# A four-layer graph network on one core: layer 2's clamps on POOL, its squares between two exponentials, and the rows' tangent from an exponential

## The chip, the core and the metric

The kernel runs on one core of one Trainium2 chip. The metric is the device time of one execution in microseconds (us). Engines are named as in the profile: PE is TensorE's matmul, PEld its weight load, DVE is VectorE, ACT is ScalarE, POOL is GpSimd, SP is SyncE.

## What is computed

A vector of 64 features for each of 4096 nodes passes four graph layers. Each layer normalizes the rows of x, clips them at zero, mixes them over a 4096x4096 adjacency matrix, and adds the result to x.

```python
h = jnp.maximum(_layernorm(x, axis=-1), 0.0)
x = x + _L2_gnn_ref(h, adj, L2_gnn_weight, L2_gnn_bias)
```

Layer 0 is a sum over neighbours with a linear map, layer 1 an attention with a sigmoid weight for each pair of nodes, and layer 3 a sum over each node's last 100 neighbours. The change is in layer 2, which takes a logarithmic map between each pair of nodes on the Poincare ball, sums it with the adjacency as weight, applies a linear map, and goes back with an exponential map:

```python
arg = jnp.clip(sqrt_c * sub_norm, 0.0, TANH_CLIP)
return 2.0 / (sqrt_c * lam_x) * jnp.arctanh(arg) * sub / sub_norm
...
agg = jnp.einsum('ij,ijc->ic', w, log_ij)
transformed = agg @ weight + bias
...
second = jnp.tanh(sqrt_c * lam_x * v_norm / 2.0) * v / (sqrt_c * v_norm)
```

Around the origin the last line is tanh(|v|) v / |v|, one tanh per row.

## The kernel before, in words

The nodes are cut into eight blocks of 512 (ib). A group is one block of 512 targets against 256 sources: a tile of 128 partitions x 2 chunks x 512, 1024 elements a partition, and 512 KB of the adjacency matrix. Layers 0, 1 and 3 have 128 groups each.

Layer 2 uses that the pair weight is symmetric but for the adjacency. Its list `work` (line 957) holds only the groups with source block J not below target block ib: 72 groups, 56 of them with J above ib ("two"), whose weights are also transposed on PE and weighed a second time for the other half. Eight groups ("cut") work on half a tile. A group goes through these steps:

- `l2_dists` (PE): float32 and bfloat16 matmuls into the PSUM tile mm give the distance expression;
- `l2_squares` (ACT): v is the square of mm; then `l2_signs` (PE) adds a term to mm;
- `l2_clamps` (line 1032, DVE): v is lowered by a constant and held above a small one, in place;
- `l2_roots` (line 1050, ACT): Ln of v in place, then t = exp(v/2), then v = exp(-v/2) in place;
- `l2_coshs` (DVE): t = max(mm, c) + t, after which mm is free; `l2_logs` (ACT): Ln of t;
- `l2_pairs` (DVE): t = min(t, top) * v; `l2_weights` (DVE): w = t * adj;
- `l2_turns` (PE) transposes t into PSUM; `l2_weights2` (DVE): two multiplies of 128x512 with the other half of the adjacency;
- `l2_sums` and `l2_sums2` (PE) add into the two accumulators; `l2_gathers` moves the turned half into the tile others.

When a target block has its last sum, `after2` (line 613) handles its rows: transposes, the linear map, the squared norm n, on POOL the powers n^0.5 and n^-0.5 by one `pow` of 128x8 (r_nn), on ACT the tanh of the norm, a reload of ACT's tables by `log_exp_tables` (line 297), and on DVE the product and the add to x. `before3` (line 532) follows with the next layernorm, whose inverse root is a POOL `pow` of 128x4 (ln_r), an add of a bias to x on POOL, and the bfloat16 splits for layer 3.

The order in which each engine gets its instructions is fixed when the kernel is built. `in_turn` (line 709) takes among generators the step that can start earliest by a model of times (`Pace`, line 59): 1.65 for a `pow` on POOL, 0.3 + n/600 for its other work, 2.6 for a reload of the tables. The steps of layer 2 that share an engine are bound together by `in_steps` (line 1212): in step s each generator does the group s minus its offset, in the order listed. ACT's list is logs (one behind), roots (level), squares (one ahead); DVE's is clamps, pairs (one behind), weights (one behind), coshs, second weights (one behind). Row work is put between these steps where the model finds it ready. The tiles v and t of the groups share six buffers. Every engine instruction of the kernel goes through one helper, so that all stand at line 129 in the profile, and groups are told apart by tile names.

Of the kernel before, what the change touches and what calls it, by code (L numbers as in the profile page):

```python
# [13 lines left out]
AF = mybir.ActivationFunctionType  # L14
# [10 lines left out]
CB = W // P  # L25
# [111 lines left out]
def kernel(ctx: ExitStack, tc: tile.TileContext, a: dict, out: bass.AP):  # L137
# [156 lines left out]
    def rt(name, shape, dtype=F32):  # L294
        return rows.tile(shape, dtype, tag=f"{name}_{slot['now']}", name=name, bufs=1)

    def log_exp_tables():

        tc.keep_in_program_order(nc.scalar.preload_act_table_set("natural_log_exp_and_others"))
        pace.free["ACT"] += 2.6  # L300
# [312 lines left out]
    def after2(ib, acc, others, st):  # L613

        e = rows.tile([P, W], F32, tag="e", name="e")[0 : D + 1, :]
        if others is None:
            ACT.copy(e, acc[0 : D + 1, :])
        else:
            DVE.tensor_add(e, acc[0 : D + 1, :], others)
        st["acc_free"][0] = pace.latest  # L620
        ps = yield from by_row(e, D + 1)

        t = rt("l2", [P, CB, D])
        z = rt("r_n", [P, CB, 1])
        DVE.tensor_copy(z, ps[:, :, D : D + 1])
        h = HA[:, cs(ib), 0:D]
        hz = rt("r_sq", [P, CB, D])
        DVE.tensor_mul(hz, h, ps[:, :, 0:D])  # L630
        DVE.tensor_mul(t, ps[:, :, 0:D], Qc[:, cs(ib), :].to_broadcast([P, CB, D]))
        yield ON_V
        y = rt("r_m", [P, CB, 1])
        DVE.tensor_reduce(y, hz, AX.X, ALU.add)
        DVE.tensor_mul(y, y, Mc[:, cs(ib), :])
        DVE.tensor_add(z, z, y)
        DVE.tensor_mul(z, z, Fc[:, cs(ib), :])
        yield ON_V
        DVE.tensor_mul(hz, h, z.to_broadcast([P, CB, D]))
        DVE.tensor_sub(t, t, hz)  # L640
        vT = columns[slot["now"]]
        yield from transposed(t, D, vT[0:D, :])
        ps = yield from times(vT, W2, D, ON_S)
        tr = rt("hb", [P, CB, D])
        ACT.copy(tr, ps)
        hz = rt("r_sq", [P, CB, D])
        ACT.activation(hz, tr, AF.Square)
        yield ON_V
        n = rt("r_nn", [P, 2 * CB, 1])
        DVE.tensor_reduce(n[:, 0:CB, :], hz, AX.X, ALU.add)  # L650
        DVE.tensor_scalar(n[:, 0:CB, :], n[:, 0:CB, :], MIN_NORM * MIN_NORM, None, ALU.max)
        DVE.tensor_copy(n[:, CB :, :], n[:, 0:CB, :])

        POOL.tensor_tensor(n, n, halves["both"], ALU.pow)
        yield ON_S
        th = rt("r_c", [P, CB, 1])
        ACT.activation(th, n[:, 0:CB, :], AF.Tanh)
        log_exp_tables()
        yield ON_V
        DVE.tensor_mul(th, th, n[:, CB :, :])  # L660
        DVE.tensor_mul(tr, tr, th.to_broadcast([P, CB, D]))
        DVE.tensor_add(x[:, cs(ib), :], x[:, cs(ib), :], tr)
        yield ON_V
# [307 lines left out]
    def targets(d):  # L971
        return slice(d["ib"] * W + (OWN if d["cut"] else 0), (d["ib"] + 1) * W)


    def ago(items, k, n, what):

        return items[k - n].get(what) if k >= n else 0.0
# [44 lines left out]
    def l2_squares():  # L1022
        for k, d in enumerate(work):
            yield "ACT", lambda: latest(
                d.get("dist"), l1[2 * k - SIG].get("summed") if 2 * k < SIG else 0.0,
                ago(work, k, SIG // 2, "paired"),
            )
            d["v"] = pair_buffer("v")
            ACT.activation(part(d, d["v"]), part(d, d["ps"]), AF.Square)
            d["square"] = pace.latest  # L1030

    def l2_clamps():
        for d in work:
            yield "DVE", lambda: d.get("square")
            v = part(d, d["v"])
            DVE.tensor_scalar(v, v, -half, V_MIN, ALU.add, ALU.max)
            d["clamped"] = pace.latest

    def l2_signs():
# [10 lines left out]
    def l2_roots():  # L1050
        for k, d in enumerate(work):
            yield "ACT", lambda: latest(
                d.get("clamped"), opened.get("tables"),
                l1[2 * k + 1 - SIG].get("summed") if 2 * k < SIG else 0.0,
                ago(work, k, SIG // 2, "weighed"), ago(work, k, SIG // 2, "turned"),
            )
            d["t"] = pair_buffer("t")
            v = part(d, d["v"])
            ACT.activation(v, v, AF.Ln)
            ACT.activation(part(d, d["t"]), v, AF.Exp, scale=0.5)  # L1060
            d["root"] = pace.latest
            ACT.activation(v, v, AF.Exp, scale=-0.5)
            d["inverse"] = pace.latest

# [7 lines left out]
    def l2_logs():  # L1072
        for d in work:
            yield "ACT", lambda: d.get("read")
            ACT.activation(part(d, d["t"]), part(d, d["t"]), AF.Ln, scale=2.0 / SC)
            d["log"] = pace.latest

    def l2_pairs():
        for d in work:
            yield "DVE", lambda: latest(d.get("log"), d.get("inverse"))  # L1080
            t = part(d, d["t"])
            DVE.scalar_tensor_tensor(t, t, top, part(d, d["v"]), ALU.min, ALU.mult)
            d["paired"] = pace.latest

    def l2_weights():
        for k, d in enumerate(work):
            yield "DVE", lambda: latest(
                opened.get("second"), d.get("paired"), arrival(d), ago(work, k, 2, "summed")
            )
            if not d["cut"]:  # L1090
                d["w"] = w2["pool"].tile([P, G, W], F32, tag="w", name="w")
            DVE.tensor_mul(part(d, d["w"]), part(d, d["t"]), part(d, d["adj"]))
            d["weighed"] = pace.latest
            used(d)
# [104 lines left out]
    def l2_gathers():  # L1199
        for d in twos:  # L1200
            if d["half"] == 0:
                continue
            yield "DVE" if d["ib"] else "ACT", lambda: d.get("summed2")
            o, acc = w2["others"][:, ws(d["J"])], accs["turned"][0 : D + 1, :]
            if d["ib"] == 0:
                ACT.copy(o, acc)
            else:
                DVE.tensor_add(o, acc, o)
            st["acc_free"][1] = pace.latest
            d["gathered"] = pace.latest  # L1210

    def in_steps(*stages):


        parts = [next(stage[0], None) for stage in stages]
        for step in range(-1, len(work) + 3):
            for n, (gen, behind, many) in enumerate(stages):
                k = step - behind
                for _ in range(many(work[k]) if 0 <= k < len(work) else 0):
                    yield parts[n]  # L1220
                    parts[n] = next(gen, None)
# [132 lines left out]
    def l3_pass():  # L1354

        for n, pair in enumerate(pairs3):
            while rank_need(pair) is None:
                yield "PE", lambda: first_of(rank_need(pair), sum_need() if sums3 else None)
                if rank_need(pair) is None:
                    l3_sum()  # L1360
            yield "PE", lambda: rank_need(pair)
            l3_rank(pair)
            for _ in range(1 + n % 2):
                if sums3 and sum_need() is not None:
                    yield "PE", sum_need
                    l3_sum()
        while sums3:
            yield "PE", sum_need
            l3_sum()

    def l3_weights():
        n = 0
        for d in l3:
            if d["late"]:
                place, reader = late_at[d["k"]]
                yield "ACT", lambda: latest(d.get("ranked"), reader.get("signed"))
                d["w"] = place
            else:
                yield "ACT", lambda: latest(
                    d.get("ranked"), opened.get("third"),  # L1380
                    ago([e for e in l3 if not e["late"]], n, WT, "summed"),
                )
                d["w"] = now["w3"].tile([P, G, W], BF16, tag="wt", name="wt")
                n += 1
            ACT.activation(d["w"].bitcast(U16), d["ps"], AF.Relu)
            d["read"] = pace.latest
# [8 lines left out]
    def l3_sum():  # L1395
# [22 lines left out]
        if d["last"]:  # L1418
# [8 lines left out]
            (l2_dists(), -1, once), (l2_signs(), 0, once), (l2_sums2(), 2, if_two(1)),  # L1427
            (l2_turns(), 1, lambda d: 2 if d["two"] else 1), (l2_sums(), 1, once),
        ),
        in_steps((l2_logs(), 1, once), (l2_roots(), 0, once), (l2_squares(), -1, once)),  # L1430
        in_steps(
            (l2_clamps(), 0, once), (l2_pairs(), 1, once), (l2_weights(), 1, once),
            (l2_coshs(), 0, once), (l2_weights2(), 1, lambda d: 2 if d["two"] else 1 if d["first"] else 0),
        ),
        l2_gathers(), l3_weights(), l3_pass(), l3_counts(), l3_masks(),
        degree_sums(0, l0), degree_sums(1, l1), constants(),
    ])

# [44 lines left out]
```

## Time and profile before

| what | value |
|---|---|
| median of the runs shown | 1198.92 us (1196.69 to 1200.99, 3 runs) |
| the profiled execution, its own time | 1196.08 us |
| its span, first to last instruction | 1194.4 us |
| busy in the span | PE 1077.9 (90%), DVE 950.6 (80%), ACT 800.7 (67%), POOL 118.2 (10%) |
| layer 2, by its first square and its last sums | about 482 to 960 us |
| clamp v<-v on DVE, 128x1024 | 64 times, mean 684 ns |
| ACT table loads | 19 times, 1283 ns |

A busy time is the sum of an engine's instructions, and engines work at the same time. A line of a timeline gives start, duration, engine, operation, out<-in with shapes, and in brackets the idle time before it and whom it waited for. A line of waits gives who waited for whom: total us, times, longest. An operation's displayed duration overlaps the next one's start by some 0.1 us on ACT and DVE, so that what it costs its queue is read from start to start.

### The profile page before, as it was taken

To read this page: it belongs to the slowest core of one execution; us is meant where nothing else is said; L and a number is where in the kernel's file an instruction comes from. 1 tells how busy PE (TensorE), PEld (TensorE's weight loads), DVE (VectorE), ACT (ScalarE), POOL (GpSimd) and SP (SyncE) were. 2 spreads that over 40 slices of the span, in tenths; PEclk is the share of its full clock that TensorE was granted. 3 is DMA by queue.
4 is the path that set the end of the run, shared out by engine and by line. 5 is a ranking of instruction groups with operands and counts; after the bars stand their busy time and mean duration, and the time that the engine had idled before them with its cause. 6 is when DMAs were issued, how large, how long until landed. Compare 5 with 4: busy or idle time off the path is not lost.

```text
span 1194.4 us, 15545 instructions
## 1 busy us (share of the span) xinstructions
PE 1077.9 (90%) x5367; PEld 445.8 (37%) x5392; DVE 950.6 (80%) x1571; ACT 800.7 (67%) x1266; POOL 118.2 (10%) x99
## 2 busy tenths in 40 slices
PE   4799999999999999899979979899878779999997
PEld 1234443333333333244434434344433333333332
DVE  7889888869988887698989989898989884555550
ACT  1055456677776766879888798788876675555554
POOL 3123222002000010000010010100010120000000
PEclk9899999999999999899999999999999899999999
DMA  8899999775767764544535535344444398888830
GB/s 307 300 409 388 405 386 329 265 244 184 249 225 244 253 241 157 193 141 159 194 106 177 176 109 198 117 159 159 159 143 141 138 357 319 314 315 310 309 112 9
DMA packets 77190, 271.75 MB, mean 228 GB/s; under 512 B 10040, under 2 KB 11064, under 8 KB 77112
## 3 DMA queue, kind: packets, MB, share of 16 engines
q1 hardware_dynamic: 75456, 270.57, 63.7%
q8 instruction: 42, 0.69, 0.2%
q10 hardware_dynamic: 1656, 0.20, 0.1%
q14 instruction: 36, 0.29, 0.1%
HBM read 269.68 MB, written 1.05 MB: 227 GB/s over the span
## 4 chain that ended last, share of the span: by engine, by line
PE 47%; DVE 25%; ACT 13%; issue 7%; DMA 5%; POOL 2%; SPq 0%; ACTq 0%; DVEq 0%; POOLq 0%
PE acc L129 23%; PE mm L129 16%; PE tr L129 8%; DVE t L129 6%; DVE w L129 6%; DVE dg L129 4%; DMA adj<-in_adjT_dram 4%; ACT wt L129 3%; ACT v L129 3%; ACT t L129 2%; DVE v L129 1%; DVE sig L129 1%; POOL lo_s L129 1%; ACT sig L129 1%; ACT lo_sq L129 1%
## 5 line engine op out<-in xcount | busy, mean ns | idle before, releaser
L129 PE MATMUL acc<-w,HA 128*65 128x256 f32 (+1 forms) x736 | 252.6, 479 | 22.2 <-DVE w L129 13.8
L129 ACT ACTIVATE wt<-mm 128x1024 uint16<-128x1024 f32 x124 | 120.4, 1020 | 93.0 <-PE mm L129 93.0
L129 ACT ACTIVATE v<-v 128x1024 f32<-128x1024 f32 (+1 forms) x144 | 145.3, 1009 | 54.5 <-DVE v L129 52.2
L129 ACT ACTIVATE sig<-mm,att_b,att_a 128x1024 f32<-128x1024 f32 x128 | 148.5, 1202 | 44.2 <-PE mm L129 43.2
L129 DVE TENSOR_TENSOR sig<-sig,adj 128x1024 f32<-128x1024 f32 x128 | 152.5, 1220 | 28.3 <-ACT sig L129 28.1
L129 PE MATMUL acc<-adj,HA 128*64 128x512 f32 x512 | 128.0, 631 | 22.9 <-DVE HA L129 19.4
L129 DVE TENSOR_TENSOR dg<-dg,adj 128x1024 f32<-128x1024 f32 x114 | 139.1, 1220 | 2.0 <-DMA adj<-in_adjT_dram 0.6
L129 PEld LDWEIGHTS acc<-w,HA 128*65 128x65 f32 x736 | 95.8, 140 | 110.5 <-issue 59.5
L129 PE MATMUL mm<-qT,kT 64*128 64x512 f32 x512 | 132.6, 632 | 3.3 <-ACT sig L129 3.3
L129 PE MATMUL acc<-sig,HL 128*64 128x512 f32 x512 | 123.5, 605 | 1.6 <-DVE sig L129 1.5
L129 PE MATMUL acc<-wt,S 128*128 128x512 bf16 (+1 forms) x480 | 98.7, 391 | 2.7 <-issue 2.4
L129 DVE SCALAR_TENSOR_TENSOR t<-t,v 128x1024 f32<-128x1024 f32 x72 | 85.4, 1186 | 5.2 <-ACT t L129 5.2
L129 DVE SCALAR_TENSOR_TENSOR t<-mm,t 128x1024 f32<-128x1024 f32 x72 | 83.3, 1157 | 4.1 <-ACT t L129 2.1
L129 DVE TENSOR_TENSOR w<-tr,adj 128x512 f32<-128x512 f32 x120 | 78.5, 683 | 10.1 <-PE tr L129 10.1
L129 DVE TENSOR_TENSOR w<-t,adj 128x1024 f32<-128x1024 f32 x72 | 83.5, 1160 | 1.2
L129 PE MATMUL tr<-ident,t 128*128 128x128 f32 x480 | 67.7, 283 | 16.7 <-DVE w L129 6.9
L129 PE MATMUL mm<-RT,LT 64*128 64x512 f32 (+1 forms) x288 | 78.9, 625 | 3.6 <-DVE t L129 3.6
L129 ACT ACTIVATE t<-t 128x1024 f32<-128x1024 f32 x72 | 72.1, 1002 | 13.3 <-DVE t L129 13.2
L129 DVE TENSOR_SCALAR RT<-adj 128x1024 bf16<-128x1024 f32 x74 | 50.4, 696 | 33.5 <-PE mm L129 31.6
L129 ACT ACTIVATE t<-v 128x1024 f32<-128x1024 f32 x72 | 72.7, 1010 | 2.3
L129 PEld LDWEIGHTS mm<-qT,kT 64*128 64x128 f32 x512 | 43.9, 189 | 75.1 <-ACT sig L129 35.2
L129 ACT ACTIVATE v<-mm 128x1024 f32<-128x1024 f32 x72 | 69.2, 961 | 0.8 <-PE mm L129 0.8
(204 smaller groups left out, 1298.4 us busy)
## 6 DMA issues: line engine op xcount, KB each, us to landing
adj<-in_adjT_dram SPq DMA_DIRECT2D x512, 512.0 KB, 4.9
x<-in_x_dram SPq DMA_DIRECT2D x4, 256.0 KB, 3.8
out_dram<-h SPq DMA_DIRECT2D x8, 128.0 KB, 2.8
b<-in_b_dram ACTq DMA_DIRECT2D x2, 32.0 KB, 5.3
W<-in_W_dram ACTq DMA_DIRECT2D x3, 16.0 KB, 4.2
W0T<-in_W0T_dram ACTq DMA_DIRECT2D x2, 16.0 KB, 5.5
W1T<-in_W1T_dram ACTq DMA_DIRECT2D x1, 16.0 KB, 4.9
W1T<-in_b_dram ACTq DMA_DIRECT2D x1, 0.2 KB
```

The source lines that it names most:

```text
L129: done = self.tc.keep_in_program_order(getattr(self.engine, op)(*args, **kw))
```

## The change

Three edits. The clamps are issued on POOL instead of DVE, as a thread of their own outside DVE's list of steps. The third activation of `l2_roots`, the exponential that makes the inverse, becomes a generator `l2_inverses` of its own, listed behind the squares, so that ACT's order within a step is log, Ln, exp, square of the next group, inverse. In `after2` the tanh of the norm becomes exp(-2n) on ACT and three operations of 128x4 on DVE, 2 / (1 + exp(-2n)) - 1, and the reload of ACT's tables after it is dropped.

```diff
         POOL.tensor_tensor(n, n, halves["both"], ALU.pow)
         yield ON_S
+
         th = rt("r_c", [P, CB, 1])
-        ACT.activation(th, n[:, 0:CB, :], AF.Tanh)
-        log_exp_tables()
-        yield ON_V
+        ACT.activation(th, n[:, 0:CB, :], AF.Exp, scale=-2.0)
+        yield ON_V
+        DVE.tensor_scalar(th, th, 1.0, None, ALU.add)
+        DVE.reciprocal(th, th)
+        DVE.tensor_scalar(th, th, 2.0, -1.0, ALU.mult, ALU.add)
         DVE.tensor_mul(th, th, n[:, CB :, :])
...
     def l2_clamps():
         for d in work:
-            yield "DVE", lambda: d.get("square")
+            yield "POOL", lambda: d.get("square")
             v = part(d, d["v"])
-            DVE.tensor_scalar(v, v, -half, V_MIN, ALU.add, ALU.max)
+            POOL.tensor_scalar(v, v, -half, V_MIN, ALU.add, ALU.max)
             d["clamped"] = pace.latest
...
             ACT.activation(part(d, d["t"]), v, AF.Exp, scale=0.5)
             d["root"] = pace.latest
+
+    def l2_inverses():
+        for d in work:
+            yield "ACT", lambda: d.get("root")
+            v = part(d, d["v"])
             ACT.activation(v, v, AF.Exp, scale=-0.5)
             d["inverse"] = pace.latest
...
-        in_steps((l2_logs(), 1, once), (l2_roots(), 0, once), (l2_squares(), -1, once)),
         in_steps(
-            (l2_clamps(), 0, once), (l2_pairs(), 1, once), (l2_weights(), 1, once),
+            (l2_logs(), 1, once), (l2_roots(), 0, once), (l2_squares(), -1, once),
+            (l2_inverses(), 0, once),
+        ),
+        in_steps(
+            (l2_pairs(), 1, once), (l2_weights(), 1, once),
             (l2_coshs(), 0, once), (l2_weights2(), 1, lambda d: 2 if d["two"] else 1 if d["first"] else 0),
         ),
-        l2_gathers(), l3_weights(), l3_pass(), l3_counts(), l3_masks(),
+        l2_clamps(), l2_gathers(), l3_weights(), l3_pass(), l3_counts(), l3_masks(),
```

## The prediction

> **What bounds the kernel now.** First the table of stretches, cut where layer 2 begins and ends. Its columns are the stretch, its length, then busy time (and instructions) of PE, PEld, DVE, ACT, POOL, then clock, DMA share and GB/s.
>
> ```profile
> 482.00:956.00 474.00, 417.53 (x1943) 195.97 (x1942) 429.64 (x627) 387.07 (x451) 29.06 (x20) 0.97 0.45 153
> 956.00:1194.00 238.00, 214.85 (x1343) 79.38 (x1364) 118.57 (x202) 133.45 (x145) 8.35 (x6) 0.98 0.70 256
> ```
>
> Layer 2 has three nearly full engines: PE is idle for 474 - 417.5 = 56.5 us, DVE for 44, ACT for 87. POOL is almost free. Whatever the change does, PE's work there stays, so no more than about 56 us can go.
>
> Second, the timeline in the middle of a block row, one group after another. PE's four pieces of a group with both halves are sums of the turned half 1.93, transposes 1.04, sums 1.9 and distances 1.5. With their overlaps the pattern repeats every 5.85 to 5.9 us (in the chain of waits the turned sums start at 726.03, 731.92 and 737.77), and PE has no gap. DVE's own list (starts to starts) is minimum-multiply 1.25, weigh 1.14, cosh 1.13, two turned weighs 1.20, clamp 0.60: 5.3, and 5.6 with half of an "others" add of 0.6. ACT's is 0.95 + 1.08 + 1.09 + 0.97 + 0.91 = 5.0. So between block ends PE sets the pace and DVE follows closely.
>
> Third, the waits in 482 to 970, by engine waiting. ACT's first line is the clamp itself, but ACT has 0.85 us to spare in each period. The PE lines are the ones to take:
>
> ```profile
> PE acc L129 <- DVE w L129: 13.8, 19, 1.4
> PE mm L129 <- ACT v L129: 11.1, 4, 2.8
> PE acc L129 <- DVE others L129: 8.1, 9, 1.9
> PE tr L129 <- DVE w L129: 6.9, 2, 4.9
> PE tr L129 <- DVE t L129: 6.5, 9, 1.8
> ...
> ACT v L129 <- DVE v L129: 52.2, 55, 4.1
> ```
>
> Fourth, where those lie. Summing PE's gaps over 0.4 us gives 10 us at the start of the layer (482 to 550) and 5.7 to 8.3 us around each of seven block ends, 46 in all. Here is the largest of one such place:
>
> ```profile
> 691.99 2.49 POOL L129 TENSOR_TENSOR r_nn<-r_nn,halves 128x8 f32<-128x8 f32 x1 [78.95 <-DVE r_nn L129]
> ...
> 693.70 1.28 ACT L129 ACT_TABLE_LOAD   x1
> 694.99 0.20 ACT L129 ACTIVATE r_c<-r_nn 128x4 f32<-128x4 f32 x1
> 695.22 1.28 ACT L299 ACT_TABLE_LOAD   x1
> 697.73 0.42 ACT L129 ACTIVATE r_sq<-ln_xc 128x256 f32<-128x256 f32 x1 [1.24 <-DVE ln_xc L129]
> 698.06 1.00 ACT L129 ACTIVATE v<-mm 128x1024 f32<-128x1024 f32 x1
> 699.11 0.39 PE L129 MATMUL mm<-RB,LB 2*128 2x512 bf16 x2 [2.77 <-ACT v L129]
> 699.95 0.73 POOL L129 TENSOR_TENSOR x<-x,b 128x256 f32<-128x256 f32 x1
> 700.04 1.72 DVE L129 SCALAR_TENSOR_TENSOR t<-t,v 128x1024 f32<-128x1024 f32 x1 [0.25 <-ACT t L129]
> ```
>
> The reader is to see two things. The square (v<-mm) stands in ACT's queue behind the tanh, its two table loads and a row square, and PE waits 2.77 us for it. And t<-t,v, elsewhere 1.22 us, takes 1.72 while POOL adds x and b: the 0.64 us that were left of POOL's 0.73 come back as 0.50.
>
> **What the Trainium skill says.** "SBUF — State Buffer", section Who interferes with whom: a DVE instruction with two SBUF inputs and a GpSimd instruction that reads SBUF exclude each other; one with at most one SBUF input, outside the two-port modes, does not. The 1.72 above agrees; so does the power of 128x4, 1.01 us when alone and 1.85 when issued during a two-input multiply. "GPSIMD Engine Reference", section Engine selection: elementwise with two inputs is about twice VectorE's time, with one input roughly line rate. The trace has no one-input operation of this size on POOL. "ScalarE: Activation LUTs", sections What ACT_TABLE_LOAD costs and Table sets: 1283 ns for a load, and Exp and Ln share one set. The trace has 1.28, and shows the next operation right behind it, without the further drain that the page adds.
>
> **The change, part by part.**
>
> *Clamps leave DVE.* 64 of 684 ns and 8 of 415; by starts they cost about 0.60 and 0.35, so 64 x 0.60 + 8 x 0.35 = 41 us of DVE over the layer, about 3.0 in the five groups around a block end.
>
> *Clamps on POOL.* The unknown price. Below: a 128x512 memset is 0.52 and 128x128 is 0.21, 0.82 ns an element; a select with one input of 128x128 took 0.30, so 0.30 + 896 x 0.82 ns = 1.03 us. Above: the select's slope from a fixed 0.10 is 1.6 ns, so 1.75; the two-input add (0.73 for 256) would even give 0.10 + 1024 x 2.4 = 2.6. I take 1.2, since the clamp has one input; I keep 1.03 and 2.6. POOL then works 72 x 1.2 = 85 us more of 474. A first glance says that 1.2 for 0.6 is a loss, but nobody pays it if it lies right. The new order on ACT is log, Ln, Exp, square of the next group, inverse; from the square's end to that group's Ln there are now the inverse 0.97 and the log 0.95, about 1.95 us, where before only the log lay. And the square runs beside the cosh, which also follows Exp; so the clamp falls beside the two turned weighs. Cosh and turned weighs read PSUM and one SBUF tile, and are not excluded. So 1.2 fits in 1.95 with the lock free: zero in the middle of a row, with PE's 5.85 as before. If that cover is gone (the clamp still runs when minimum-multiply is due), DVE waits up to 1.2, of which 0.55 to 0.85 is slack.
>
> *Squares between the exponentials.* No instruction is added. The inverse moves 1 us later, but its reader waits for the log behind it anyway: zero.
>
> *Tangent from an exponential.* 16 loads of 1.28 = 20.5 us leave ACT; three operations of 128x4 join DVE, 0.17 + 0.18 + 0.17 with their hand-overs 0.6 per block. They lengthen the rows' chain, which the next groups don't read, but DVE's queue stands behind it. The wait for the power (2.49) was partly hidden under the first load and now shows.
>
> *What is queued behind POOL.* Five POOL operations per block (the powers and the x+b add) now meet clamps. A clamp behind a power is up to 2.5 late; of this 0.75 + 0.85 is slack. The rows' powers wait up to 1.2 for a clamp, and DVE and ACT, which run in a fixed order, stand with them. No DMA is moved, but SP's loads wait for DVE's weighs and follow them.
>
> **The sum, against the profiled 1196.08 (span 1194.4).**
> - The 2.77 gaps: four shown, and the same pattern at the three later ends (under other names: 1.29 + 1.80, part of 4.88): 7 x 2.77 = 19.4. I keep 80%, 15.5, since the power's wait returns some.
> - The last rows, after the layer: a load is on the chain once (977.48, 1.28): 1.3.
> - The other PE gaps at block ends, (46 - 19.4) / 7 = 3.8 each, are for DVE. It loses 3.0, gains 0.6, and I give 1.0 to collisions with clamps (five clamps, one in three meeting a wait of about 0.6): net 1.4, so 7 x 1.4 = 9.8.
> - Start of the layer: 10 us idle, partly for clamps behind the rows' work: 1.
> - Middle of rows: 0.
> Together 27.6; layer 3 is PE-bound and begins that much earlier. 1196.1 - 27.6 = 1168.5. The median of the runs shown, 1198.92, lies 2.8 above the profiled one, so I state 1171.3, rounded 1171.
>
> **Rivals.** About 0.3% (3.6 us) is what a measurement of this kernel can tell from no change.
> - *The lock takes the relief back* (chance 0.18). Clamps fall on two-input operations whenever DVE lags, each costing DVE what it lost; only the table loads count, and half of them: 1198.9 - 11 = 1188. For: the 1.72. Against: the cover worked out above.
> - *The clamp is late* (0.15): the slower side, one mechanism in the middle of rows. Let L be the time from the square's end to the clamp's end. A period cannot be shorter than L + Ln 1.08 + Exp 1.09 + square 1.0 = L + 3.15, so from L = 2.7 it exceeds PE's 5.85. If POOL first waits for a weigh (1.2) and then runs 2.0, L is 3.2: 64 x 0.5 = 32 us lost, less 17 from the loads: 1214. For: price and lock are unmeasured here. Against: at 1.2 even with that wait L is 2.4.
> - *Nearly every gap closes* (0.08): 45 of 56 us, 1154. Against: short block rows keep latency that no engine's load explains.
> - *No change* (0.05): other waits take the places, and the planner, which prices a POOL clamp at 2.0, puts row work at worse places: 1197.
>
> **Numbers.** The forecast, 1158 to 1186, has 0.54. Faster: 0.54 + 0.08 + 0.16 of the first rival = 0.78. Same: 0.05 and 0.01 = 0.06. Slower: 0.15 and 0.01 = 0.16. The range 1154 to 1203 leaves out most of the late clamp (0.13) and the half of the third rival below 1154 (0.04).
>
> **What would show it.** Right: table loads fall from 19 to 3; v<-v on POOL near 1.2; the 2.77 gaps under 0.6; ACT's wait for the clamp under 15 us; PE still 5.85 in mid-row; layer 3 unchanged in length. Wrong: clamps of 2 us or more, t<-t,v or w<-t,adj with a mean above 1.4, mid-row periods over 6.0, or ACT waiting for POOL as long as it did for DVE.

## The result, and the profile after

| | before | after |
|---|---|---|
| median of four runs | 1197.81 us (1196.58 to 1200.99) | 1231.04 us (1230.06 to 1234.02) |
| ratio to before, 95% interval | | 1.0272 (1.0242 to 1.0302) |
| profiled execution, its span | 1196.08, 1194.4 | 1234.02, 1232.3 |
| layer 2, first square to last square | 482.55 to 942.32: 459.8 | 485.19 to 977.23: 492.0 |
| table loads on ACT | 19 | 3 |

The change is 33 us slower. The forecast was 1171, the range ended at 1203. The two profiled spans differ by 37.9 us: 32.3 lie between layer 2's first and last square, 2.6 ahead of them and 3.0 behind. The medians differ by 33.2, since the profiled execution after is the longest of its four; so the 32.3 are nearly all there is to explain. The mean granted clock was lower as well, 0.967 against 0.978, but that is not what makes the 32.3: the loop found below holds no PE operation, and makes 33.8. In layer 3 nothing else happens than before, as the table of stretches shows (columns as before: stretch, length, busy PE, PEld, DVE, ACT, POOL, clock, DMA share, GB/s):

```profile
482.00:994.00 512.00, 435.05 (x1965) 203.25 (x1964) 409.30 (x579) 370.09 (x451) 286.26 (x93) 0.95 0.42 143
994.00:1232.00 238.00, 213.25 (x1332) 78.14 (x1355) 117.80 (x203) 127.59 (x139) 8.76 (x6) 0.98 0.70 256
```

PE's idle time in layer 2 has grown from 56 to 77 us. No engine is as full as before (PE 85%, DVE 80%, ACT 72% of the stretch; before 88%, 91% and 82%), and POOL went from 29 us to 286. The page of the changed kernel, its shares of the chain that ended last and some groups (busy us, mean ns of one, idle time ahead and who ended it):

```profile
span 1232.3 us, 15629 instructions
PE 1091.4 (89%) x5367; PEld 453.9 (37%) x5392; DVE 927.9 (75%) x1523; ACT 775.0 (63%) x1250; POOL 375.5 (30%) x171
...
PE 39%; POOL 20%; issue 16%; DVE 12%; ACT 10%; DMA 3%; ACTq 0%; SPq 0%; POOLq 0%; DVEq 0%
...
L129 POOL TENSOR_SCALAR v<-v 128x1024 f32<-128x1024 f32 x72 | 254.7, 3537 | 217.6 <-ACT v L129 217.6
...
L129 DVE SCALAR_TENSOR_TENSOR t<-t,v 128x1024 f32<-128x1024 f32 x72 | 85.7, 1190 | 11.1 <-ACT t L129 11.1
...
L129 DVE TENSOR_TENSOR w<-t,adj 128x1024 f32<-128x1024 f32 x72 | 84.5, 1174 | 1.8
```

Two readings. The clamp on POOL takes 3.54 us in the mean of both sizes (64 of 128x1024 at 3739 ns, 8 of half that at 1920), not 1.2. And t<-t,v and w<-t,adj nearly kept their means (1186 and 1160 ns before), which lie under the 1.4 that the prediction named as a sign of the lock.

An engine that is busy 30% of the span holds 20% of the chain. The timeline of one group in the middle of a row shows how (start, duration, engine, operation, in brackets the idle time before it):

```profile
646.90 1.02 ACT L129 ACTIVATE v<-mm 128x1024 f32<-128x1024 f32 x1
647.03 1.22 DVE L129 SCALAR_TENSOR_TENSOR t<-mm,t 128x1024 f32<-128x1024 f32 x1 [0.50 <-ACT t L129]
647.81 1.04 ACT L129 ACTIVATE v<-v 128x1024 f32<-128x1024 f32 x1
648.00 3.63 POOL L129 TENSOR_SCALAR v<-v 128x1024 f32<-128x1024 f32 x1 [3.18 <-ACT v L129]
648.75 1.04 ACT L129 ACTIVATE t<-t 128x1024 f32<-128x1024 f32 x1
649.83 1.23 DVE L129 SCALAR_TENSOR_TENSOR t<-t,v 128x1024 f32<-128x1024 f32 x1 [0.38 <-ACT t L129]
651.66 1.06 ACT L129 ACTIVATE v<-v 128x1024 f32<-128x1024 f32 x1 [1.86 <-POOL v L129]
652.75 1.06 ACT L129 ACTIVATE t<-v 128x1024 f32<-128x1024 f32 x1
653.71 1.00 ACT L129 ACTIVATE v<-mm 128x1024 f32<-128x1024 f32 x1
654.80 3.63 POOL L129 TENSOR_SCALAR v<-v 128x1024 f32<-128x1024 f32 x1 [3.17 <-ACT v L129]
```

It is a ring: the clamp ends at 651.63, ACT starts this group's Ln at 651.66, then its Exp, then the next group's square, and only then POOL can clamp again. Nothing in it waits for PE or DVE. Between 648.00 and 654.80 lie 3.63 of clamp and 3.17 in which POOL waits for those three activations: the period is 6.80, not 5.85. ACT stands idle for 1.86 us in each period, just ahead of Ln. In the kernel before, the group whose square starts at 653.71 above has its clamp on DVE, of 0.68:

```profile
633.85 1.01 ACT L129 ACTIVATE v<-mm 128x1024 f32<-128x1024 f32 x1
...
635.84 0.68 DVE L129 TENSOR_SCALAR v<-v 128x1024 f32<-128x1024 f32 x1
...
636.56 1.06 ACT L129 ACTIVATE v<-v 128x1024 f32<-128x1024 f32 x1 [0.76 <-DVE v L129]
...
639.70 1.01 ACT L129 ACTIVATE v<-mm 128x1024 f32<-128x1024 f32 x1
```

From square to square that is 5.85, PE's own pace. The chain of waits of the changed kernel shows the ring without any reading of engines; it alternates the clamp and ACT's part, which this view calls "issue":

```profile
641.19 3.63 POOL v L129
644.82 3.14 issue
...
648.00 3.63 POOL v L129
651.62 3.13 issue
...
654.80 3.63 POOL v L129
```

Of the 71 intervals from square to square, 36 lie at 6.75 to 6.85. Those 36 sum to 245.0 us, and in the kernel before the same ones sum to 211.2: 33.8 us more. The other 35, with the block ends where the gain was forecast, are together only 1.5 us shorter. So the loss is the ring in the middle of rows, and nearly nothing was gained elsewhere. The waits of layer 2 (who waited for whom: total us, times, longest; 482 to 1000):

```profile
POOL v L129 <- ACT v L129: 217.6, 67, 20.2
ACT v L129 <- POOL v L129: 84.6, 52, 4.0
...
DVE t L129 <- ACT t L129: 60.0, 61, 3.1
...
PE mm L129 <- DVE t L129: 29.6, 27, 6.8
```

POOL waits for ACT and ACT for POOL: two engines that wait for each other in turn, and neither is full (POOL works 3.63 us of each 6.80). PE's waits bear DVE's name, but DVE waited 60 us for ACT. The engine named beside PE's wait is the last link only.

### The profile page after: what moved, and what is told of

Its sections match the earlier page's. It is cut to its first block, busy times and chain, and to the rows that moved or that the text cites. A ratio compares the mean times of both kernels' runs of the same rounds, so it can differ in the third digit from the quotient of the medians.

```text
span 1232.3 us, 15629 instructions
## 1 busy us (share of the span) xinstructions
PE 1091.4 (89%) x5367; PEld 453.9 (37%) x5392; DVE 927.9 (75%) x1523; ACT 775.0 (63%) x1250; POOL 375.5 (30%) x171
## 4 chain that ended last, share of the span: by engine, by line
PE 39%; POOL 20%; issue 16%; DVE 12%; ACT 10%; DMA 3%; ACTq 0%; SPq 0%; POOLq 0%; DVEq 0%
PE acc L129 18%; POOL v L129 17%; PE mm L129 14%; PE tr L129 7%; DVE dg L129 3%; ACT wt L129 3%; DMA adj<-in_adjT_dram 3%; ACT v L129 2%; ACT t L129 1%; DVE sig L129 1%; POOL ln_r L129 1%; DVE w L129 1%; POOL lo_s L129 1%; ACT sig L129 1%; DVE t L129 1%
## 5 line engine op out<-in xcount | busy, mean ns | idle before, releaser
L129 POOL TENSOR_SCALAR v<-v 128x1024 f32<-128x1024 f32 x72 | 254.7, 3537 | 217.6 <-ACT v L129 217.6
L129 PE MATMUL acc<-w,HA 128*65 128x256 f32 (+1 forms) x736 | 261.2, 493 | 25.8 <-DVE w L129 15.4
L129 PEld LDWEIGHTS acc<-w,HA 128*65 128x65 f32 x736 | 98.5, 145 | 118.5 <-issue 59.4
L129 PE MATMUL mm<-qT,kT 64*128 64x512 f32 x512 | 129.5, 619 | 3.3 <-ACT sig L129 3.3
L129 DVE SCALAR_TENSOR_TENSOR t<-mm,t 128x1024 f32<-128x1024 f32 x72 | 83.6, 1161 | 62.7 <-ACT t L129 48.9
L129 PE MATMUL acc<-wt,S 128*64 128x512 bf16 (+1 forms) x479 | 98.4, 390 | 3.2 <-issue 2.9
L129 DVE SCALAR_TENSOR_TENSOR t<-t,v 128x1024 f32<-128x1024 f32 x72 | 85.7, 1190 | 11.1 <-ACT t L129 11.1
L129 POOL TENSOR_TENSOR ln_r<-ln_v,minus_half 128x4 f32<-128x4 f32 x32 | 51.5, 1608 | 139.5 <-DVE ln_v L129 139.5
```

What stands on the lines that cost most here:

```text
L129: done = self.tc.keep_in_program_order(getattr(self.engine, op)(*args, **kw))
```

## The experiments

Ratios are to the kernel before, timed on the same chip. The theory after the result: *the price* (POOL's clamp is dear in itself, and the ring's period is clamp + 3.17). The rivals: *the lock* (POOL and DVE exclude each other, so that each is slowed by the other), and *the other edits* (the squares' order or the tangent harm).

**clamp_dve.** The changed kernel with only the clamps put back on DVE, first in its list.

```diff
-            yield "POOL", lambda: d.get("square")
+            yield "DVE", lambda: d.get("square")
...
-            POOL.tensor_scalar(v, v, -half, V_MIN, ALU.add, ALU.max)
+            DVE.tensor_scalar(v, v, -half, V_MIN, ALU.add, ALU.max)
```

> The changed kernel with its clamps back on DVE; the tangent and the order of the squares stay as changed. Late clamp (theory): the loss is POOL's 3.63 us per clamp, so mid-row periods return from 6.80 to 5.85 and the time falls below the kernel before, to about 1185 (16 table loads and their gaps gone). Planner's order (rival): the row work that the other two edits move makes the loss, so about 1215 or more and periods over 6.2 stay.

Measured: 1187.23 us, 0.9929 (0.9900 to 0.9958). The 36 intervals of mid-row are back at a mean of 5.85 (before: 5.87). The clamps' place alone costs 1231.0 - 1187.2 = 43.8 us; the other two edits together gain some 8. The rival *the other edits* falls.

**tangent_only.** The kernel before with only the tangent from an exponential (the three DVE operations, no reload of tables).

> The kernel before with the tangent's edit alone. If the table loads set the 2.77 us gaps of PE as the prediction said: 3 loads in place of 19, the four gaps under 1 us, time 1180 to 1186. If the loads were hidden under the wait for the power and ACT then waits for that instead: 1195 to 1199.

Measured: 1198.62, 0.9989 (0.9970 to 1.0008): no difference, though 16 loads are gone. The prediction's largest term, 15.5 us, came from these loads. The same block end as in the prediction, in this kernel:

```profile
691.10 2.49 POOL L129 TENSOR_TENSOR r_nn<-r_nn,halves 128x8 f32<-128x8 f32 x1 [77.81 <-DVE r_nn L129]
...
693.61 0.20 ACT L129 ACTIVATE r_c<-r_nn 128x4 f32<-128x4 f32 x1 [0.83 <-POOL r_nn L129]
693.73 1.00 ACT L129 ACTIVATE v<-mm 128x1024 f32<-128x1024 f32 x1
693.85 0.17 DVE L129 TENSOR_SCALAR r_c<-r_c 128x4 f32<-128x4 f32 x1 [0.64 <-ACT r_c L129]
...
695.54 0.68 DVE L129 TENSOR_TENSOR w<-tr,adj 128x512 f32<-128x512 f32 x1
...
696.92 0.68 DVE L129 TENSOR_TENSOR w<-tr,adj 128x512 f32<-128x512 f32 x1
697.66 1.94 PE L129 MATMUL acc<-w,HA 128*65 128x256 f32 x8 [2.21 <-DVE w L129]
```

The square now starts right behind the tangent's exponential, and PE's gap of 2.77 behind it is gone. In its place PE waits 2.21 for the turned weighs. They stand on DVE behind the tangent's three operations, which wait for the power on POOL, and behind the rows' two multiplies and the sum; the next norm's mean and its subtraction lie between the two weighs. In the kernel before, nearly the same queue lay under the loads. There the second weigh was

```profile
697.62 0.68 DVE L129 TENSOR_TENSOR w<-tr,adj 128x512 f32<-128x512 f32 x1
```

It ended at 698.30, only 0.8 us ahead of the end of the square that PE waited for. The trace of the kernel before had shown that little could be won there.

**clamp_split.** The changed kernel with one chunk of each clamp on POOL and the other on DVE.

```diff
+            v = part(d, d["v"])[:, 0]
             POOL.tensor_scalar(v, v, -half, V_MIN, ALU.add, ALU.max)
...
+            v = part(d, d["v"])[:, 1]
+            DVE.tensor_scalar(v, v, -half, V_MIN, ALU.add, ALU.max)
```

> The changed kernel with one chunk of each clamp (128x512) on POOL and the other on DVE. Late clamp: POOL takes 1.92 us as it did for the half tiles, L + 3.15 = 5.1 is below PE's 5.85, so mid-row is 5.85 again and the time 1180 to 1195. Shared port (rival): POOL and DVE exclude each other as often as with the full clamp, minimum-multiplies or weighs rise to a mean of 1.3 us or more, and the time stays above 1205.

Measured: 1192.80, 0.9960 (0.9942 to 0.9978). POOL's halves take 1982 ns in the mean, and the pace of 6.8 is gone from mid-row. t<-t,v and w<-t,adj have means of 1.16 and 1.19, so the lock's forecast of 1.3 or more fails. In total it is no faster than clamp_dve (0.9929), but the two parts of the layer differ. From the eighteenth square on it takes 341.3 us against clamp_dve's 348.6, so there relief of DVE does pay. The first seventeen intervals take 116.9 against 104.4; two of them last 12.1 and 11.1, and in each PE waits for ACT's copy of the turned sums (others), 4.68 and 3.68 us.

**prices.** Most of the kernel is left out: no layer is computed, and only operations of POOL on tiles of the clamp's size run, first alone, then beside DVE.

> The disputed prices by themselves; the four layers are left out and the output is not theirs. POOL operations of one and of two steps, with one and two inputs, at 256, 512 and 1024 elements while DVE is idle, then four clamps beside a row of two-input multiplies on DVE, then four beside two-port scalar operations. If 3.63 us is POOL's own price: 3.6 for 1024 and about 1.9 for 512 alone, and a slope of 3.3 ns an element. If it comes from the shared port: about 1.2 alone and 3 or more in company. One step may take half of what two take, about 1.9.

Measured, the groups alone (L76 lowers and bounds, L79 bounds only, L82 adds two tiles, L85 copies) and beside a run of two-input multiplies on DVE (L91); columns: busy us, mean ns of one, idle before:

```profile
L76 POOL TENSOR_SCALAR lone<-src 128x1024 f32<-128x1024 f32 x2 | 7.3, 3626 | 0.2
L79 POOL TENSOR_SCALAR lone<-src 128x1024 f32<-128x1024 f32 x2 | 5.5, 2765 | 0.2
L82 POOL TENSOR_TENSOR lone<-src,xin 128x1024 f32<-128x1024 f32 x2 | 4.7, 2338 | 0.2
...
L85 POOL COPY lone<-src 128x1024 f32<-128x1024 f32 x2 | 2.1, 1042 | 0.1
...
L91 POOL TENSOR_SCALAR crowd<-lone 128x1024 f32<-128x1024 f32 x4 | 16.1, 4031 | 0.3
```

The clamp takes 3.63 alone, the same as in mid-row of the changed kernel: DVE has no part in it, and the lock falls as the main cause. Beside a full DVE it takes 0.4 more. The prediction had reasoned from the number of inputs, and of these forms only the copy fits it: 1.04 for one input. A scalar operation with one input is dearer than an add with two, and its second step costs 0.9 us. What DVE loses beside a clamp, from the timeline of the same kernel:

```profile
43.34 1.94 DVE L89 TENSOR_TENSOR one<-three,four 128x1024 f32<-128x1024 f32 x1
45.20 0.21 DVE L93 TENSOR_TENSOR two<-three,four 128x64 f32<-128x64 f32 x1
45.34 1.21 DVE L89 TENSOR_TENSOR one<-three,four 128x1024 f32<-128x1024 f32 x1
```

Clamps run here without a pause from 42.67 on. The first multiply is 0.73 us late; the next one, still under the same clamp, is not.

**squares_only.** The kernel before with only the new order of ACT (the inverse behind the next square).

> The kernel before with the squares' order alone (square ahead of the inverse; clamps on DVE, tanh and its table loads kept). If the earlier square is what gained 11.6 us in the kernel with the clamps back on DVE: about 1187, as the tangent alone gave nothing. If it takes both edits (the tables' reload stands between the exponential and the square otherwise): 1194 to 1199.

Measured: 1194.81, 0.9963 (0.9945 to 0.9980). Slightly faster, where the prediction had zero, and within the second of the two ranges expected. Its interval overlaps clamp_dve's, so how much of clamp_dve's gain is this edit's stays open.

**clamp_only.** The kernel before with only the clamps on POOL, so with ACT's old order, in which the inverse lies ahead of the next square.

> The kernel before with its clamps on POOL alone; the square stays behind the inverse and the tanh stays. Late clamp: the loop is then clamp 3.63, Ln, Exp, inverse and square, 3.63 + 3.17 + 0.97 = 7.8 us a group, 1.0 more than in the changed kernel over 64 groups, so about 1231 + 62 = 1293. Occupation (rival: POOL's work itself or the port sets the loss, whatever the order on ACT): about 1231, as the changed kernel.

Measured: 1301.39, 1.0853 (1.0820 to 1.0886). Its clamps in mid-row:

```profile
659.20 3.62 POOL L129 TENSOR_SCALAR v<-v 128x1024 f32<-128x1024 f32 x1 [4.26 <-ACT v L129]
667.09 3.62 POOL L129 TENSOR_SCALAR v<-v 128x1024 f32<-128x1024 f32 x1 [4.26 <-ACT v L129]
```

The period is 7.89: one activation more in the ring, 1.09 longer. The rival, the same loss whatever ACT's order, falls. So the squares' move is worth some 70 us when the clamp is on POOL (1301.4 to 1231.0; the tangent, worth nothing alone, is the other difference) and 4 when it isn't: it took an activation out of the ring that the other edit had closed.

**clamp_one.** The changed kernel with a cheaper clamp on POOL: one step (the bound), and the subtraction as the bias of Ln on ACT.

```diff
-            POOL.tensor_scalar(v, v, -half, V_MIN, ALU.add, ALU.max)
+            POOL.tensor_scalar(v, v, half + 2.0**-63, None, ALU.max)
...
-            ACT.activation(v, v, AF.Ln)
+            ACT.activation(v, v, AF.Ln, bias=lower)
```

> The changed kernel with a clamp of one step on POOL: max of the square and a floor, while the subtraction becomes the bias of Ln. POOL's price alone was 2.77 us for this form, so the loop is 2.77 + 3.17 + 0.1 for the bias = 6.0, against PE's 5.85: late clamp gives 64 x 0.8 = 51 us less than the changed kernel, about 1182 to 1192. Rival (port): clamps still lie on the minimum-multiplies, above 1205.

Measured: 1194.60, 0.9967 (0.9956 to 0.9978), 2.6 us above the range expected. Its mid-row:

```profile
643.44 2.77 POOL L129 TENSOR_SCALAR v<-v 128x1024 f32<-128x1024 f32 x1 [3.27 <-ACT v L129]
649.48 2.77 POOL L129 TENSOR_SCALAR v<-v 128x1024 f32<-128x1024 f32 x1 [3.27 <-ACT v L129]
```

The period is 6.04: the clamp is 0.86 shorter, the period 0.76. The price theory stands; the ring is nearly as short as PE's 5.85. The range had all 64 groups at the ring's pace; the 36 that keep it give 27.5 us, all others together 10. Against clamp_dve this kernel is 4.9 us shorter from the eighteenth square on (343.8 to 348.6) and 6.3 longer in the first seventeen intervals.

**clamp_add.** The changed kernel with an add of a constant tile on POOL in the clamp's place. The subtraction and the bound are left out.

```diff
-            POOL.tensor_scalar(v, v, -half, V_MIN, ALU.add, ALU.max)
+            POOL.tensor_tensor(v, v, floor.to_broadcast([P, *v.shape[1:]]), ALU.add)
```

> The changed kernel with an add of a constant in place of the clamp (both its subtraction and its bound are left out), as a two-input operation on POOL, 2.34 us alone. Loop 2.34 + 3.17 = 5.5, below PE's 5.85: late clamp gives mid-row periods of 5.85 and, as DVE has no clamps, a time at or under that with the clamps back on DVE: 1178 to 1188. If the periods stay at 6 or more, the loop isn't all of it.

Measured: 1197.18, 0.9982 (0.9967 to 0.9996), outside what was expected. Mid-row is as expected (the operation takes 1.90 with the small second operand, the period is 5.85, PE has no gap). At block ends it is not:

```profile
698.31 1.92 POOL L129 TENSOR_TENSOR v<-v,floor 128x1024 f32<-128x1024 f32 x1 [1.52 <-ACT v L129]
...
698.51 2.01 DVE L129 TENSOR_TENSOR hb<-hb,r_c 128x256 f32<-128x256 f32 x1
```

DVE's multiply of 0.42 takes 2.01: it ends 0.3 after the POOL operation. The same happens at four of the eight block ends. Here the lock is real and covers nearly the whole operation. Of VectorE's two-port modes "SBUF — State Buffer", section Who interferes with whom, of the Trainium skill says that whichever of the two issues first has the shared ports for the whole instruction. This pair, a multiply of two SBUF inputs beside an add, behaves in that way. The clamp does not: a DVE operation that it holds loses 0.7 to 0.85 us of its 3.6, in the timelines of prices and of the changed kernel. So a shorter operation on POOL was no better at block ends: eight intervals around one take 51.4 us here and 51.6 in clamp_dve. The lock isn't the whole miss. Of the 9.7 us by which the profiled span exceeds clamp_dve's, 5.5 lie ahead of layer 2 and 3.9 in its first seventeen intervals. The granted clock of the first 100 us was 0.90 here and 0.95 there; whether it made the 5.5 was not tried.

**no_clamp.** The changed kernel without any clamp (the bound is left out; Ln gets a tiny bias). This is what a clamp that costs nobody anything would give.

> The changed kernel without any clamp (its subtraction and its bound are left out; Ln gets a tiny bias), so that neither DVE nor POOL does it. The prediction counted a hidden clamp as free and came to 1171. If only POOL's price was wrong in it: 1165 to 1177. If the gains it counted at block ends are not there either: 1180 to 1190, like the kernel with the clamps back on DVE, with PE gaps of 2 us left at the block ends.

Measured: 1178.63, 0.9841 (0.9810 to 0.9872). So even a free clamp gives some 19 us (15 to 23), between the two ranges expected and not the 27.6. From the eighteenth square on, the layer is 27.8 us shorter than before (354.7 to 326.9); the first seventeen intervals are 5.8 longer. One of those is 13.9 us: ACT's copy of the turned sums (others) stands behind four activations of 128x1024, and PE waits 5.22 us for it. That is an order that the kernel's own model of times chose. The four kernels in which POOL's clamp is cheaper, halved or absent (clamp_one, clamp_add, clamp_split and no_clamp) all lose here: their first seventeen intervals take 108.3 to 116.9 us, against 105.1 before and 104.4 in clamp_dve.

**no_clamp_tanh.** no_clamp with the tanh and its two loads put back.

> The changed kernel without any clamp (the logarithm gets a tiny bias instead; the bound is left out), and with the rows' tangent back as a tanh with its two table loads. Without the clamps, and with the tangent from an exponential, the kernel took 1178.6. Theory 'the loads are covered once by the turned weighs, whatever DVE has to do': the loads are worth no more than they were beside the clamps on DVE (0 to 4 us): 1179 to 1183, with new gaps of PE at block ends below 1.5 us each. Theory 'the loads count once DVE is relieved', the prediction's own term: 7 x 2.77 x 0.8 = 15.5 us come back: 1191 to 1196, with gaps of 2.8 us behind the square.

Measured: 1176.81, 0.9822 (0.9794 to 0.9849), the same as no_clamp within the intervals. The second theory falls: the loads are worth next to nothing with DVE relieved either. A block end (eight intervals of squares) takes 48.9 here and 47.5 in no_clamp, against 52.2 before: the loads do cause a gap of PE there, of 1.45 us. But from first to last square the layer is only 1.8 us longer with them (439.6 to 437.8), where the prediction had 15.5.

**dve_pow26, dve_pow34 and one_told.** These follow from tangent_only: DVE's row work is put ahead of the turned weighs because the model prices the 128x8 power at 1.65 us, while it takes 2.49 beside a multiply. In dve_pow26 and dve_pow34 clamp_dve's model is told 2.6 and 3.4; in one_told clamp_one's is told 2.6, and 0.2 + n/400 for the clamp.

```diff
+            if str(self.name(out)).startswith("r_nn"):
+                return 2.6
```

> Clamps back on DVE, tangent and squares as changed, and the planner's price for the rows' power of 128x8 raised from 1.65 to 2.6, near the 2.49 it takes. The tables' 2.77 gaps had become 2.2 behind the turned weighs, which stand on DVE behind the row work that waits for the power. If that order is the cause: the turned weighs go first, the four 2.2 gaps shrink below 1, and the time falls to about 1178 to 1184. If the gap is made by DVE's work itself: 1186 to 1192 again.

> The same with the planner's price at 3.4 us, the power and the hand-overs on both sides of it. If the order is the cause, at least as good as 2.6: 1176 to 1184; if row work is only pushed to another bad place, 1186 or more.

> The clamp of one step on POOL (the subtraction as Ln's bias), with the planner told POOL's true prices: 2.6 for the power of 128x8, 0.2 + n/400 for the clamp. Mid-row stays at 6.03 a group, 0.18 above PE's 5.85, so late clamp leaves 64 x 0.18 = 12 us in it; the order at block ends may give 5 to 8 back: 1186 to 1191. If it reaches the kernel with clamps on DVE and the same price of the power, the loop's excess costs nothing.

Measured: 1182.91, 0.9883 (0.9858 to 0.9909); 1189.99, 0.9935 (0.9910 to 0.9960); 1191.00, 0.9940 (0.9917 to 0.9964). In dve_pow26 the turned weighs go ahead of the rows' work at the block end, and the gap of 2.2 becomes one of 1.44 before the transposes. Its line there is

```profile
694.38 1.06 PE L131 MATMUL tr<-ident,t 128*128 128x128 f32 x8 [1.44 <-DVE t L131]
```

The time lies in the range for order as the cause, though the gap isn't under 1. It is the fastest kernel here that computes everything, 4 to 6 us under clamp_dve, with intervals that just overlap. dve_pow34 came out in its second range: PE waits 1.77 us at another place, for DVE's sum of the turned half (others), and the kernel is 2.9 us longer than dve_pow26 between first and last square and 3.0 behind it. So a higher price is not always better; no run followed that further. one_told is at the upper edge of its range, and its order gave nothing within the layer: 454.4 us from first to last square, as in clamp_one. It doesn't reach dve_pow26, so nothing shows that the ring's excess is free.

## Why the prediction was wrong

**The failed step is the price in "Clamps on POOL".** It says "I take 1.2, since the clamp has one input; I keep 1.03 and 2.6". The measured price is 3.63, three times the value and above the upper end. Both ends came from other kinds of operation: a memset, a select, an add. The clamp is a scalar operation with two steps, and no row of the profile before had one on POOL. The page of the Trainium skill that supported the choice, "GPSIMD Engine Reference", section Engine selection, says one input is roughly line rate; the copy agrees (1.04 us for 1024 elements), the scalar operation does not (2.77 with one step, 3.63 with two). The two-input add, from which the 2.6 came, takes 2.34 alone, so the upper end was fair for its own kind and not for the clamp's. It matters, because at 2.6 L is 2.68, still under the turning point of 2.7: by itself no price in the range made the ring longer than PE's 5.85. An upper end for an operation that no row shows has to be left open, or measured.

**The mechanism was the second rival, "the clamp is late".** It gave the period as L + 3.15 and the turning point as L = 2.7. In mid-row the square starts at 646.90 and ends at 647.92, the clamp ends at 651.63: L = 3.71, so 6.86, and 6.80 was measured. Over the kernels:

| kernel | POOL's operation, us | period by L + 3.15, with L = operation + 0.08 | measured |
|---|---|---|---|
| clamp_add | 1.90 | 5.13, so PE's 5.85 | 5.85 |
| clamp_one | 2.77 | 6.00 | 6.04 |
| after | 3.63 | 6.86 | 6.80 |
| clamp_only (an inverse of 0.97 more) | 3.63 | 7.83 | 7.89 |

The 0.08 is the time from the square's end to the clamp's start. The rival's time of 1214 had L = 3.2 and 64 groups, less 17 for the loads. With L = 3.71 the same sum gives 64 x (6.86 - 5.85) - 17 = 48 us lost. Measured were 33: only 36 intervals keep the ring's pace, and the loads' 17 did not come. Its chance of 0.15 rested on the price again ("at 1.2 even with that wait L is 2.4").

**The terms of the sum, had the price been right.**

- *The 2.77 gaps, 15.5 us, and the last rows, 1.3.* Wrong by nearly all. The gap behind the square went as described, but the turned weighs were next to be late, by 2.2 (tangent_only: no difference). The prediction named the cause ("The wait for the power (2.49) was partly hidden under the first load and now shows", "DVE's queue stands behind it") and took off 20% for it; it was nearly 100%.
- *DVE's relief, 9.8.* This is net: 3.0 for each block end, 21 in all, less 0.6 each for the tangent's operations and 1.0 each for collisions with clamps. no_clamp_tanh has neither of the two. It is 1.78% faster than before, 21.3 us; less squares_only's 0.37%, 4.4 us, that leaves 17 if the two add up. So the 21 was of the right size. It isn't the relief alone that is measured here: the clamp's time between square and Ln is gone too. The 7.0 for collisions stays unmeasured.
- *Squares between the exponentials, zero.* 4 us (squares_only).
- *The start of the layer, +1.* Not shown to be a gain: 5.8 us lost in no_clamp, where one copy stands in a bad place.
- *Middle of rows, zero.* This holds for clamp_add and no_clamp, at 5.85. For the real clamp it is the loss.

A free clamp has no collisions, so its forecast would have been 27.6 + 7.0 = 34.6, against some 19 measured. Without the loads' 16.8 it is 17.8. That this comes near the 19 is luck in part: the squares' 4 us and the 5.8 lost at the start of the layer are not in it, and pull in opposite directions. That no_clamp's 1178.6 lies inside the forecast's 1158 to 1186 is luck of the same kind.

**The first rival, the lock,** didn't decide. In mid-row t<-t,v of 649.83 starts 1.83 us into a clamp and takes its usual 1.23. Of the 144 operations t<-t,v and w<-t,adj one is held by a clamp, at a block end: w<-t,adj at 934.57 takes 2.05 beside a clamp that began at 934.34. Four more take 1.75 beside POOL's add of x and b, as they did before (1.72).

**What the prediction had right:** PE's 5.85 in mid-row as the bound that the ring must stay under, table loads from 19 to 3, layer 3 unchanged, and the signs of failure: clamps over 2 us and mid-row periods over 6.0 are what came.

## What to carry to other kernels

An operation moved to an idle engine is not free because the engine is: if a tile goes engine A, B and back to A, and the next tile's step on A stands in A's queue behind the return, the links form a loop. Its period is the sum of the links, and it decides as soon as it passes the busiest engine's period, though neither of the two engines is full. Whether a square issued two groups ahead would break the loop here was not tried. Write that sum down with the worst price for the moved operation before the best, and measure the very form (kind, number of steps, size) alone if no row shows it. When a stall is taken from a queue that a full engine feeds, look for what stood in that stall's shadow: here it was as long as the stall.

## What the runs showed of the hardware

- On POOL, 128x1024 in float32: copy 1.04 us, add of two tiles 2.34 (1.90 with a small repeated second operand), scalar operation with one step 2.77, with two 3.63. From the 128x512 forms (1.92 and 1.49), each further element costs 3.3 ns with two steps and 2.5 with one.
- DVE operations held by a two-step scalar operation on POOL lost 0.7 to 0.85 us each, out of its 3.6, and then ran beside it (prices: 1.94 for 1.21 at 43.34, 2.04 at 51.77; after: 2.05 for 1.22 at 934.57). In prices three of four clamps held one operation, and the last held two of DVE's scalar operations, at 55.48 and 58.05 (1.52 and 1.53 for 0.68). A two-input add on POOL held a two-input multiply for nearly its whole 1.9 (clamp_add, four block ends).
- The mean granted TensorE clock was 0.978 before, 0.967 after and 0.948 in clamp_only, and PE's busy time was 1077.9, 1091.4 and 1121.5 us for the same products. It was also 0.968 in clamp_add, where PE has no gap in mid-row, so a wait of PE in every period isn't needed for a low one. The cause wasn't tried apart.
- Executions of one kernel differ with that clock: of 13 of the kernel before, timed together, the shortest (1192.10 us) had 0.981 and the longest (1203.72) 0.967.
